# A graph layer on one core: where the edge count, the last store and the gathered blocks stand in the program

## The chip, the cores and the metric

The kernel runs on one core of one Trainium2 chip, in one launch. A core has TensorE (PE: matmuls, with a separate row PEld for its weight loads), VectorE (DVE), ScalarE (ACT), GpSimd (POOL) and SyncE (SP). They run side by side, each takes its own instructions strictly in order, and they wait for each other on semaphores. DMAs are issued from the queues of SP, ACT and POOL.

The metric is device time in microseconds (us): the median of several executions.

## The reference

One layer of a graph network over 6250 nodes of 128 features and 100,000 edges that are sorted by destination. Every edge carries its source's row through one of two weight matrices, by its type; the messages are summed by destination; the node's own row through a third matrix is added; then ReLU, the residual and a normalisation of each row.

```python
Xs = X[src]
m_data = Xs @ W_data.T + b_data
m_ctrl = Xs @ W_control.T + b_control
msg = jnp.where((edge_types == 0)[:, None], m_data, m_ctrl)
agg = jax.ops.segment_sum(msg, dst, num_segments=X.shape[0])
out = agg + (X @ W_self.T + b_self)
return jax.nn.relu(out)
# and around it
x = _layernorm(x + _L0_gnn_ref(x, ...), axis=-1)
```

## The kernel before

**Stages.** The nodes are cut into 49 blocks of 128. First a table of messages is built: every node times both edge matrices, split into three bf16 parts (384 columns a row), kept in SBUF (`m3`) and stored to DRAM (`table`). Then each destination block takes the edges that can belong to it, a window of 2304 sorted edges (KT = 18 columns of 128), and sums the messages of those edges. There are two ways of doing that.

- 35 blocks ("p", seven groups of five) go by *windows*. DVE and PE rank the edges of a group by the source's table block (`acc`, `slot`, `two`, `small`). The result, `packed`, is sent to DRAM and read back spread over all partitions (`rows`). Then each of 25 steps per block selects rows of `m3` with a matmul (`g_ps`, L754, steps "g"), ACT or DVE copies them out of PSUM as bf16 (`gs`, L769, steps "e"), and a second matmul adds them up by destination with a one-hot matrix (`agg`, L232, steps "s"). For the last group DVE shares those copies; before it only ACT does them. Edges that found no place are put on a short list and fetched by an indirect DMA into `mixed` (steps "over" to "spilled"). The step "full" (L701) takes what did not fit from that group's column of `counts`.
- 14 blocks ("g") are *gathered*: POOL fetches the message of each edge from `table` by indirect DMA (`msg`, L854, 14 x 18 of them, five buffers), and a matmul with a one-hot matrix (`hot_g`) adds them up (`agg_g`, steps "gm"). These are spread through the work of the windows.

Each finished block is summed from its three parts (`whole`, L153), gets the residual (`h_p` or `h_g`, L149) and its mean and variance (`stats`, L163, L164). `normalise` takes several blocks together, a piece of them: DVE writes `v` (L168), ACT takes its square root (L170), DVE makes `rstd` and `shift` in six small operations (L176 to L184), ACT applies them block by block (L190), and `store_out` stores the piece (L197, and L202 for the last, short block). The last two pieces of the windows are four blocks and one block of the last group; the last piece of the gathered blocks has four.

**What sets the order.** Nothing is ordered by hand. Each part is a generator that yields steps; a step has a name, a cost by engine and the steps that it needs. A planner (`Order.run`) keeps a clock for every engine: it finds the earliest start that any step could have, and among the steps of that engine that could start within 0.1 us of it takes the one with the lowest due time (`due`). The instructions of a step are then issued at that place of the program. So costs and due times only decide the order of each engine's instructions; on the chip they run as semaphores allow. Two constants set the due times of the second half: BLOCK (13.1) for a block of windows and PACE (1.75) for a gather. PACE is also the cost of a gather on POOL in the plan.

```python
if kind in ("p", "g") and i[0] in ("root", "rooted", "scale", "apply", "out"):
    n = i[1] + 1
    return BUILT + 10 + (BLOCK * sum(p[2] for p in PIECES[:n]) if kind == "p" else PACE * KT * GQ * n)
```

**The end.** `counts` (128 partitions x 8) holds how many edges every group, and the gathered blocks together, have taken in. After the last planned step a matmul with ones (L919) sums it over the partitions, DVE sums the eight columns (L921) and writes the integer `total` (L922). Then every engine loads `total` (L210) and branches (L211): if it isn't 100,000, a slower way over all edges (`sums_over_all`) runs; else it is jumped over, and the closing waits and barriers of the program follow (L1040). With these inputs it is jumped over.

Of the kernel before, what the change touches and what calls it, by code (L numbers as in the profile page):

```python
# [9 lines left out]
F32 = mybir.dt.float32  # L10
# [3 lines left out]
ALU = mybir.AluOpType  # L14
AX = mybir.AxisListType
# [4 lines left out]
P = 128  # L20
# [17 lines left out]
NPG = len(GROUPS)  # L38
NPB = sum(GROUPS)
NG = NB - NPB  # L40
STARTS = [sum(GROUPS[:i]) for i in range(NPG)]
# [59 lines left out]
def step(name, costs, *needs, lag=0.0):  # L101
    return as_tuple(name), costs, [as_tuple(n) for n in needs], lag
# [6 lines left out]
@with_exitstack  # L109
def kernel(  # L110
    ctx: ExitStack,
    tc: tile.TileContext,
    x: bass.AP,
    xt: bass.AP,
    edges: bass.AP,
    w: bass.AP,
    bias: bass.AP,
    out: bass.AP,
):

    nc = tc.nc  # L140
    dram = ctx.enter_context(tc.tile_pool(name="dram", bufs=1, space=DRAM))
    const = ctx.enter_context(tc.tile_pool(name="const", bufs=1))
    table = dram.tile([NT * P, D3], BF16, name="table")
    packed = dram.tile([NPB, NT * R], BF16, name="packed")
    total = const.tile([1, 1], I32, name="total")

    def finish(h, agg, xs):

        nc.vector.scalar_tensor_tensor(h, agg, 0.0, xs, op0=ALU.max, op1=ALU.add)  # L149

    def add_parts(agg, work):
        whole = work.tile([P, D], F32, name="whole")
        nc.vector.tensor_reduce(whole, agg.rearrange("p (i c) -> p c i", i=3), axis=AX.X, op=ALU.add)  # L153
        return whole

    def load_rows(b, work, name="xs", bufs=2):
        xs = work.tile([P, D], F32, name=name, bufs=bufs)
        nc.sync.dma_start(xs, x[b * P : (b + 1) * P, :])
        return xs

    def stats(mv, h, work):
        st = work.tile([P, 6], F32, name="st")
        nc.vector.bn_stats(st, h)  # L163
        nc.vector.bn_aggr(mv, st)  # L164

    def root(mv, n, work):
        v = work.tile([P, Q], F32, name="v")
        nc.vector.tensor_scalar_add(v[:, :n], mv[:, :n, 1], EPS)  # L168
        s0 = work.tile([P, Q], F32, name="s0")
        nc.scalar.activation(s0[:, :n], v[:, :n], AF.Sqrt)  # L170
        return v, s0

    def scale(mv, v, s0, n, work):

        r0 = work.tile([P, Q], F32, name="r0")
        nc.vector.reciprocal(r0[:, :n], s0[:, :n])  # L176
        q = work.tile([P, Q], F32, name="q")
        nc.vector.tensor_mul(q[:, :n], v[:, :n], r0[:, :n])
        nc.vector.tensor_add(q[:, :n], q[:, :n], s0[:, :n])
        rstd = work.tile([P, Q], F32, name="rstd")  # L180
        nc.vector.reciprocal(rstd[:, :n], q[:, :n])
        nc.vector.tensor_scalar_mul(rstd[:, :n], rstd[:, :n], 2.0)
        shift = work.tile([P, Q], F32, name="shift")
        nc.vector.scalar_tensor_tensor(shift[:, :n], mv[:, :n, 0], -1.0, rstd[:, :n],  # L184
                                       op0=ALU.mult, op1=ALU.mult)
        return rstd, shift

    def apply(h, rstd, shift, n):
        for j in range(n):
            nc.scalar.activation(h[:, j, :], h[:, j, :], AF.Identity,  # L190
                                 bias=shift[:, j : j + 1], scale=rstd[:, j : j + 1])

    def store_out(h, b0, n):
        n0 = b0 * P
        full = min(n, (N - n0) // P)
        if full:
            nc.sync.dma_start(  # L197
                out[n0 : n0 + full * P, :].rearrange("(b p) f -> p b f", p=P), h[:, :full, :]
            )
        if full < n:  # L200
            n1 = n0 + full * P
            nc.sync.dma_start(out[n1:N, :], h[: N - n1, full, :])  # L202

    norm = stats, root, scale, apply, store_out

    with ExitStack() as main:
        sums_over_windows(main, tc, x, xt, edges, w, bias, table, packed, total,
                          add_parts, finish, load_rows, norm)

    matched = nc.values_load(total[0:1, 0:1])  # L210
    with tc.If(matched != E), ExitStack() as rest:  # L211
        sums_over_all(rest, tc, xt, edges, w, bias, table, dram, finish, load_rows, norm)


def sums_over_windows(ctx, tc, x, xt, edges, w, bias, table, packed, total,
# [166 lines left out]

    LEAD, BUILT = 8.0, 76
    BLOCK = 13.1
    PACE = 1.75
    AHEAD, FIRST = 26.0, 20

    def due(kind, *i):
# [3 lines that stand above are left out]
        if kind in ("counted", "turned", "first"):  # L392
            return 5.0
        if kind == "idx":
            return BUILT - 4
        if kind in ("stores", "built"):
            return BUILT - 6
        each = (BUILT - 8 - LEAD) / NB
        if kind == "xt":
            return LEAD - 6 + each * at_part[i[0]]  # L400
        if kind == "er":
            return 5.0
        if kind in ("set", "slots"):
            return 14.0
        if kind == "counts":
            return 9.0 if i[0] == GROUPS[0] else 30.0
        if kind == "set2":
            return 40.0
        kinds = ("y", "yh", "y1", "ym", "y2", "yl")
        if kind in kinds:  # L410
            return LEAD + each * i[0] + kinds.index(kind)
        if kind == "table":
            return LEAD + each * (at_part[i[0]] + PARTS[i[0]]) + 14
        if kind in ("win", "xs", "agg", "o", "whole", "sum"):
            b = i[0]
            begun = BUILT + (BLOCK * b if b < NPB else PACE * KT * (b - NPB))
            if kind == "win":
                return due("fields", blocks[b][0]) - 8 if b < NPB else BUILT - 20
            if b >= NPB:
                return begun + {"whole": PACE * KT + 2, "sum": PACE * KT + 5}.get(kind, 0)  # L420
            return begun + {"whole": BLOCK + 0.5, "sum": BLOCK + 3}.get(kind, 0.3 * BLOCK)
        if kind in ("rows", "sel", "d", "g", "e", "s"):
            of = {"rows": 1, "sel": 1, "d": 2}.get(kind, NS)
            lead = {"rows": -9, "sel": -3, "d": -1, "g": 0, "e": 1, "s": 2}[kind]
            return BUILT + BLOCK * (i[0] + (i[1] / of if len(i) > 1 else 0)) + lead
        if kind in ("gh", "gm", "msg"):
            k = i[1] * CH if kind == "gh" else i[1]
            return BUILT + PACE * (i[0] * KT + k) + {"msg": 0, "gh": 2, "gm": 5}[kind]
        n = GROUPS[i[0]]
        end = BUILT + BLOCK * STARTS[i[0]] - (AHEAD if i[0] else FIRST)  # L430
        span = BLOCK * n if i[0] else 34.0
        begun = end - span
        if kind == "fields":
            return begun - 8
        if kind == "hot":
            return begun + span * i[1] * KC / KT - 4
        if kind in ("tri", "rank", "rest"):
            return begun + span * i[1] / KT + {"tri": 0, "rank": 0.5, "rest": 1}[kind]
        if kind in ("two", "v"):
            c, k = (i[1], 0) if kind == "two" else divmod(i[1], KC)  # L440
            return begun + span * (c + 1) * KC / KT + (2 if kind == "two" else 3 + 0.3 * k)
        return end + ("vs", "vd", "to", "over", "pos", "codes", "posed", "list", "listed",
                      "spilled", "full").index({"packed": "vs"}.get(kind, kind))
# [370 lines left out]
    def normalise(pieces, last):  # L814

        for grp, (get, b0, q0, n) in enumerate(pieces):
# [6 lines left out]
            scales = scale(mv, v, s0, n, work)  # L823
            yield step((last, "apply", grp), {"A": 0.28 * n}, (last, "scale", grp))
            apply(h, *scales, n)
            yield step((last, "out", grp), {"S": 0.3}, (last, "apply", grp))
            store_out(h, b0, n)


    gathered = [(j, k) for j in range(NG) for k in range(KT)]  # L830
# [59 lines left out]
            stats(mv[:, j % GQ, :], h[:, j % GQ, :], work)  # L890


    late = ps_g = None

    def close_build():
# [8 lines left out]
        spread(), select(), finish_blocks(),  # L904
        normalise([(lambda g=g: (hs_[g], mvs[g]), STARTS[g] + q0, q0, n) for g, q0, n in PIECES], "p"), add_up(), gather(), evict(), to_hots(), bucket_hots(),
        multiply(), take(0, "yh", "y"), leave(0, "y1", "yh"),
        take(1, "ym", "y1"), leave(1, "y2", "ym"), take(2, "yl", "y2"), constants(), store(), close_build(),
        finish_gathered(), gathered_sums(), gathered_hots(), gather_rows(), gathered_fields(),
        normalise([(lambda i=i: kept[i], NPB + i * GQ, 0, min(GQ, NG - i * GQ))
                   for i in range(-(-NG // GQ))], "g"),  # L910
# [3 lines left out]
        own_of(list(range(NPB, NB)), lambda b: ("gm", b - NPB, 0)),  # L914
    ], due)


    total_ps = ps_a.tile([P, 512], F32, name="small")
    T.matmul(total_ps[:1, : NPG + 1], ones[:, 0:1], counts, start=True, stop=True)  # L919
    total_f = work.tile([1, 1], F32, name="total_f")  # L920
    V.tensor_reduce(total_f, total_ps[:1, : NPG + 1], axis=AX.X, op=ALU.add)  # L921
    V.tensor_copy(total, total_f)  # L922


def sums_over_all(ctx, tc, xt, edges, w, bias, table, dram, finish, load_rows, norm):
# [118 lines left out]
```

## Time and profile before

| what | us |
|---|---|
| median of 3 executions | 632.7 (629.24 to 637.61) |
| the profiled execution: its own time | 545.63 |
| its span, first to last instruction | 543.9 |
| its mean granted TensorE clock | 0.989 |
| first and last g_ps matmul | 79.9 and 530.0 |
| first and last msg gather of POOL | 89.0 and 520.4 |
| last agg_g matmul starts | 527.3 |
| `total` written | 536.0 |
| last store (out<-h_p) issued by SP | 536.5 |

The profile is of one execution, taken by the hardware profiler. A row of a group view names the line, the engine, the operation, and what is written from what, by the program's names. A row of a chain or of a timeline begins with its start and its length in us; "issue" is time in which the engine waited for nothing that the profile shows. A wait is put down to what came last. The engine names with a q (PEldq, DVEq, SPq) are the engines' sequencers, which handle branches, register loads and semaphores.

Over the whole span the page gives busy shares: PE 93%, PEld 81%, DVE 78%, ACT 78%, POOL 54%; and for the 16 DMA engines a mean of 146 GB/s.

### The profile page before, as it was taken

How to read it: one execution, taken by the hardware profiler on the slowest of the kernel's cores; microseconds unless marked ns; L12 is line 12 of the kernel's file. 1: busy time of each engine (PE TensorE's matmuls, PEld its weight loads, DVE VectorE, ACT ScalarE, POOL GpSimd, SP SyncE). 2: the span in 40 equal slices, each digit the busy share in tenths (PEclk: the TensorE clock that was granted, in tenths of full speed). 3: DMA queues.
4: the chain of work that ended last, by engine and by line, in shares of the span. 5: the costliest groups of instructions: out<-in, count | busy, mean ns of one | idle time of the engine just before them, and what ended most of it. 6: DMA issues, size and time to landing. Idle time of an engine off the chain costs nothing.

```text
span 543.9 us, 26402 instructions
## 1 busy us (share of the span) xinstructions
PE 504.0 (93%) x11222; PEld 440.7 (81%) x11222; DVE 425.9 (78%) x958; ACT 422.6 (78%) x1012; POOL 296.4 (54%) x267
## 2 busy tenths in 40 slices
PE   4899978999899999999999999999999999979990
PEld 3555538799789999898998989989988898869990
DVE  4677679778887889888799788988798766867872
ACT  6745556697778888879879797798789987978782
POOL 1000004776766667767487576676677556676610
PEclk9999989999999999999999999999999999999996
DMA  3466984444454443645445445444355542646211
GB/s 110 134 178 189 285 278 136 147 142 124 138 149 154 140 128 128 174 124 156 139 137 153 134 140 169 155 147 118 114 179 169 160 140 62 194 143 189 91 46 30
DMA packets 60934, 79.20 MB, mean 146 GB/s; under 512 B 15761, under 2 KB 51372, under 8 KB 60808
## 3 DMA queue, kind: packets, MB, share of 16 engines
q1 hardware_dynamic: 47253, 48.95, 28.0%
q0 software_dynamic: 12400, 25.08, 16.9%
q10 hardware_dynamic: 1154, 3.41, 1.8%
q8 instruction: 89, 1.46, 1.1%
q14 instruction: 38, 0.30, 0.2%
HBM read 64.35 MB, written 13.05 MB: 142 GB/s over the span
## 4 chain that ended last, share of the span: by engine, by line
PE 72%; DMA 11%; DVE 9%; ACT 3%; issue 2%; SPq 1%; POOL 1%; DVEq 0%; ACTq 0%; POOLq 0%
PE agg L232 23%; PE g_ps L754 22%; PE acc L232 8%; PE small L600 7%; PE agg_g L232 7%; DMA msg<-table,idx 5%; DMA rows<-packed 5%; PE y L460 2%; DVE hot_st L546 2%; DVE slot L563 1%; ACT gs L769 1%; ACT h_p L190 1%; PE y L478 1%; DVE rows L725 1%; ACT h_g L190 1%
## 5 line engine op out<-in xcount | busy, mean ns | idle before, releaser
L769 ACT CAST gs<-g_ps 128x384 bf16<-128x384 f32 x807 | 334.3, 495 | 71.3 <-PE g_ps L754 58.2
L854 POOL DMA_INDIRECT msg<-table,idx x252 | 285.9, 1135 | 133.7 <-PE g_ps L754 64.9
L754 PE MATMUL g_ps<-m,rows 128*32 128x384 bf16 x3430 | 319.1, 331 | 0.0
L232 PE MATMUL agg<-gs,hot_d 128*32 128x384 bf16 x3360 | 298.2, 329 | 3.7 <-ACT gs L769 3.2
L754 PEld LDWEIGHTS <-rows 128*32 128x32 bf16 x3430 | 187.2, 136 | 16.8 <-issue 10.1
L232 PEld LDWEIGHTS <-hot_d 128*32 128x32 bf16 x3500 | 188.8, 137 | 11.4 <-issue 6.8
L232 PE MATMUL agg_g<-msg,hot_g 128*32 128x384 bf16 x1008 | 108.0, 329 | 7.2 <-DMA msg<-table,idx 6.8
L563 DVE TENSOR_REDUCE slot<-acc 128x5 bf16<-128x490 f32 x126 | 83.5, 663 | 36.3 <-PE acc L232 28.3
L739 DVE TENSOR_TENSOR hot_d<-count,to 128x1664 bf16<-128x1664 bf16 x70 | 74.7, 1068 | 8.1 <-PE agg L232 7.9
L600 PE MATMUL small<-hot_st,two 128*32 128x98 bf16 x1260 | 72.5, 290 | 0.0
L600 PEld LDWEIGHTS <-two 128*32 128x32 bf16 x1260 | 59.1, 117 | 3.6 <-issue 1.4
L232 PEld LDWEIGHTS <-hot_g 128*32 128x32 bf16 x1008 | 53.0, 124 | 11.0 <-issue 9.4
L232 PE MATMUL acc<-hot_st,rest 128*32 128x490 bf16 x476 | 54.4, 376 | 7.9 <-DVE slot L563 7.8
L232 PE MATMUL acc<-hot_st,tri 128*32 128x490 bf16 x504 | 60.5, 375 | 1.1 <-DVE hot_st L546 1.1
L471 ACT CAST m<-y 128x512 bf16<-128x512 f32 (+1 forms) x75 | 40.6, 580 | 26.1 <-PE y L478 18.8
L694 POOL DMA_INDIRECT mixed<-table,row_i x7 | 8.2, 1169 | 86.5 <-PE g_ps L754 80.5
L546 DVE TENSOR_TENSOR hot_st<-count,st_b 128x2940 bf16<-128x2940 bf16 x21 | 41.9, 1999 | 7.7 <-PE small L600 6.3
L725 DVE TENSOR_SCALAR rows<-rows,pid 128x3136 bf16<-128x3136 bf16 x35 | 37.2, 1062 | 6.0 <-DMA rows<-packed 6.0
L232 PEld LDWEIGHTS <-rest 128*32 128x32 bf16 x476 | 21.7, 97 | 17.8 <-issue 16.3
L460 PE MATMUL y<-w_sb,xt 128*128 128x256 f32 x98 | 31.3, 407 | 1.8 <-DMA xt<-in_xt 1.8
L153 DVE TENSOR_REDUCE whole<-agg 128x128 f32<-128x384 f32 x35 | 19.3, 552 | 12.3 <-PE agg L232 9.2
L769 DVE CAST gs<-g_ps 128x384 bf16<-128x384 f32 x33 | 18.0, 555 | 12.9 <-PE g_ps L754 12.4
(140 smaller groups left out, 426.2 us busy)
## 6 DMA issues: line engine op xcount, KB each, us to landing
rows<-packed SPq DMA_DIRECT2D x35, 784.0 KB
table<-m SPq DMA_DIRECT2D x10, 768.0 KB
msg<-table,idx POOLq DMA_INDIRECT x252
xt<-in_xt ACTq DMA_DIRECT2D x5, 512.0 KB
xt_p<-in_xt SPq DMA_DIRECT2D x35, 64.0 KB
xs_p<-in_x SPq DMA_DIRECT2D x35, 64.0 KB
out<-h_p SPq DMA_DIRECT2D x6, 320.0 KB
table<-m SPq DMA_DIRECT2D x2, 480.0 KB
```

The costliest lines, as they stand in the source:

```text
L153: nc.vector.tensor_reduce(whole, agg.rearrange("p (i c) -> p c i", i=3), axis=AX.X, op=ALU.add)
L232: T.matmul(out[c : c + 32], lhsT[:, c : c + 32], rhs, **flags)
L460: T.matmul(y[:, j, :], xts[g][:, b + j - at_part[g], :], w_sb[:, : 2 * D], start=j == 0, stop=False, skip_group_check=True)
L471: A.copy(part_of(b, n, i), ys[b][:, :n, :].rearrange("p b (t c) -> p t b c", t=2))
L546: V.tensor_tensor(hot, counted[n][:, None, 1 : NT + 1, :].to_broadcast([P, KC, NT, n]), fields[grp][2][:, c * KC : c * KC + KC, None, :].t ...
L563: V.tensor_reduce(slots[grp][:, k, :], by_q, axis=AX.X, op=ALU.max)
L600: T.matmul(vt[c0 : c0 + R, q // 2, :], two[:, k % KC, i, :, q], hot[:, k % KC, :, q], start=k == 0 and q < 2, stop=k == KT - 1, skip_group ...
L725: V.tensor_scalar(rows[b], rows[b], pid1, None, op0=ALU.is_equal)
L739: V.tensor_tensor(hot, counted[DC][:, :, :n], places[grp][:, q, None, c * DC : c * DC + n].to_broadcast([P, P, n]), op=ALU.is_equal)
L754: T.matmul(g_ps[t * R : (t + 1) * R, :D3], rows[b][:, :, s], m3[:, s, :], start=True, stop=True)
L769: (A.copy if e == "A" else V.tensor_copy)(gs[at], g_tiles.pop((b, g))[at, :D3])
L854: G.indirect_dma_start(out=msgs[j, k], out_offset=None, in_=table[:, :], in_offset=bass.IndirectOffsetOnAxis(ap=idx[:, j, k : k + 1], axis=0),
```

## The change

Three edits to the end of the program.

1. `PACE` goes from 1.75 to 1.68.
2. The sum of `counts` becomes two planned steps, "total" on PE and "totalled" on DVE, in a generator `add_counts` of their own. They need the last group's "full" and "listed", the first one-hot tile of the second block of the last group, and the gathered blocks' count ("idx"). Their due time is that of the last block of windows. The same three instructions after the plan go away.
3. `store_out` takes the queue as an argument. The last piece of the windows is stored from ACT's queue, planned on ACT with a cost of 0.4; all other pieces from SP's, as before.

```diff
-    def store_out(h, b0, n):
+    def store_out(h, b0, n, by=nc.sync):
         n0 = b0 * P
         full = min(n, (N - n0) // P)
         if full:
-            nc.sync.dma_start(
+            by.dma_start(
...
-    PACE = 1.75
+    PACE = 1.68
...
+        if kind in ("total", "totalled"):
+            return BUILT + BLOCK * (NPB - 1)
...
-            yield step((last, "out", grp), {"S": 0.3}, (last, "apply", grp))
-            store_out(h, b0, n)
+            at_end = last == "p" and grp == len(pieces) - 1
+            yield step((last, "out", grp), {"A": 0.4} if at_end else {"S": 0.3}, (last, "apply", grp))
+            store_out(h, b0, n, nc.scalar if at_end else nc.sync)
...
+    def add_counts():
+        yield step("total", {"T": 0.2}, ("full", NPG - 1), ("listed", NPG - 1), ("d", STARTS[-1] + 1, 0), "idx")
+        total_ps = ps_a.tile([P, 512], F32, name="small")
+        T.matmul(total_ps[:1, : NPG + 1], ones[:, 0:1], counts, start=True, stop=True)
+        yield step("totalled", {"V": 0.35}, "total")
+        total_f = work.tile([1, 1], F32, name="total_f")
+        V.tensor_reduce(total_f, total_ps[:1, : NPG + 1], axis=AX.X, op=ALU.add)
+        V.tensor_copy(total, total_f)
...
-        take(1, "ym", "y1"), leave(1, "y2", "ym"), take(2, "yl", "y2"), constants(), store(), close_build(),
+        take(1, "ym", "y1"), leave(1, "y2", "ym"), take(2, "yl", "y2"), constants(), store(), close_build(), add_counts(),
...
-
-    total_ps = ps_a.tile([P, 512], F32, name="small")
-    T.matmul(total_ps[:1, : NPG + 1], ones[:, 0:1], counts, start=True, stop=True)
-    total_f = work.tile([1, 1], F32, name="total_f")
-    V.tensor_reduce(total_f, total_ps[:1, : NPG + 1], axis=AX.X, op=ALU.add)
-    V.tensor_copy(total, total_f)
```

## The prediction

> **What bounds the kernel now.** I read the page's head first, then the stretches by time, then the chain of waits of the last microseconds, then the instructions of the line that ends the program.
>
> The head says that TensorE is the engine to watch:
>
> ```profile
> span 543.9 us, 26402 instructions
> ...
> PE 504.0 (93%) x11222; PEld 440.7 (81%) x11222; DVE 425.9 (78%) x958; ACT 422.6 (78%) x1012; POOL 296.4 (54%) x267
> ```
>
> The stretches say where TensorE stops being the bound: it is busy for 9.96 us of the 10 us of the last block of windows, and for 0.31 us of the 13 us after it. The third column is PE's busy time, then PEld, DVE, ACT, POOL.
>
> ```profile
> 521.30:531.30 10.00, 9.96 (x226) 8.46 (x218) 7.85 (x25) 8.52 (x22) 0.05 (x1) 1.00 0.13 38
> 531.00:544.00 13.00, 0.31 (x10) 0.15 (x5) 3.47 (x19) 2.33 (x7) 0.00 (x0) 0.68 0.12 31
> ```
>
> So there are two different limits: about 450 us in which TensorE sets the pace, and a tail of 12.6 us (531.3 to 543.9) in which it has nothing to do. The chain of waits tells the first half of the tail (start, length, what):
>
> ```profile
> 531.38 0.54 DVE whole L153
> 531.92 0.10 DVE r L176
> ...
> 532.84 0.17 DVE shift L184
> 533.01 0.03 issue
> 533.04 1.65 ACT h_g L190 x4
> 534.68 0.10 ACT s L170
> ...
> 535.97 0.49 ACT h_p L190
> ```
>
> The last block (h_p) has to be summed, scaled and stored. But six small DVE operations for the last gathered blocks (r L176 to shift L184, 531.83 to 533.00) stand between its two steps on DVE, and four ACT operations for the same blocks (h_g, 1.65 us) stand ahead of its square root on ACT. Both are work of other blocks on the last block's path.
>
> The second half is the end of the program: after `total` is written (L922, 536.04 + 0.14), all engines load it (L210) and branch on it (L211). The view of that line (operation, count, ns min/median/max, start):
>
> ```profile
> L211 ACTq COMPARE_BRANCH  x1: 45/45/45, 536.7 to 536.7; - x1
> L211 DVEq COMPARE_BRANCH  x1: 76/76/76, 536.8 to 536.8; - x1
> L211 PEldq COMPARE_BRANCH  x1: 4171/4171/4171, 536.8 to 536.8; - x1
> L211 DVEq EVENT_SEMAPHORE  x1: 21/21/21, 540.5 to 540.5; - x1
> L211 PEldq EVENT_SEMAPHORE  x1: 51/51/51, 541.1 to 541.1; - x1
> ```
>
> TensorE's branch takes 4.17 us; DVE's takes 0.08 us, but its next instruction starts 3.58 us later. TensorE ended its sums at 531.3 and could have done this from then on; it sat waiting for `total` until 536.2, because DVE counts last of all.
>
> [...] 4.17 us on PE, 3.58 us on DVE after L211, against 0.40 us on ACT[...]. [...] SP issued the last store at 536.49, 0.03 us after ACT's last result (535.97 + 0.49). So the move of the store is worth about nothing by itself.
>
> **The change part by part.** The changed kernel's instruction order, which can be read from its build, says what moves.
>
> *Gathered blocks sooner (PACE 1.75 to 1.68).* It adds and removes no sum. Due times and planned costs of the 252 gathers shrink, so the last of the 14 gathered blocks ends about two window blocks sooner in TensorE's order: the last two blocks have no agg_g left. On DVE the gathered scale now stands in the block before last, on ACT the four h_g activations stand some 40 instructions before the end, and SP stores h_g before the last h_p. From the tail: DVE's second step (h_p, L149) started at 532.92; it can now start 0.05 us after `whole` ended (531.92), at 531.97: 0.95 us less. From there to `shift` took 3.02 us (532.92 to 535.94), of which ACT's square root was late: v ended at 533.94, the root began at 534.59 behind h_g, a gap of 0.65; in the gathered chain just before, the gap from v to the root was 0.12. So 0.53 us less again. Sum: **1.5 us**; shift then ends at 534.45.
>
> *Edges counted earlier.* The matmul of counts (two passes, 0.20 us of PE time together), the reduction (0.15) and the cast (0.14) move into the stretch of block 31, behind work that is not waiting: +0.2 us on PE at the most, +0.3 on DVE, which is idle for a fifth of that stretch (DVE 78%). On the path they leave 0.24 us (535.94 to 536.18). Their larger effect is on the branches. PE loads at 531.3 (0.49), branches (4.17) and is done at 536.0 instead of 541.0. SP and POOL, whose last DMAs are issued long before the end, load and branch while the sums still run. DVE is now last: load 534.5 to 535.0, branch, 3.58 us of fetch, next instruction at 538.7 instead of 540.5. ACT: apply ends at 534.95, store issue 0.4, load 0.46, 0.45 for its branch and what follows: 536.3. What is behind them: the closing semaphores of SP took from 540.7 to 542.1; those that do not wait for DVE can now run early. After DVE's release SP needs 0.2 us for the last ones and then the 1.86 us that ran from 542.08 to 543.93 before: 538.75 + 0.2 + 1.86 = 540.8. If the 0.9 us between SP's last two drains in that stretch also lies beside DVE's fetch, it is 539.8. Bounds of the unknown: [...] 2 to 3.7 us for it; the end then lies between 538.5 and 540.9. I take 540.3: **3.6 us** from the tail in all, 1.5 of them from the first part and 2.1 from the second.
>
> *Last store on ACT's queue.* The issue (0.36 us on SP) goes to ACT; nothing is behind it but ACT's load of `total`, which ends 2.4 us ahead of DVE's fetch. SP is freed to branch early, counted above. By itself **0**; from -0.1 (a hop saved) to +0.1.
>
> *What it costs further up.* Two things, both on TensorE's side. First, with gathered sums closer together, POOL's spacing shrinks from 1.72 us ((520.4 - 89.0) / 251) to about 1.65; a gather is busy 1.135 us and the next follows 0.30 later, so 1.43 is its floor. That holds, with less slack. TensorE waited 6.8 us in all for gathered rows (8 waits); by nearness I allow 0 to +4 more, and take +0.5. Second, the two last blocks lose their fill. TensorE then needs 49.5 x 0.1625 + 0.6 = 8.6 us for one block; by the order ACT has about 16 evictions (0.413 each), 4 applies (0.41) and a root in each, 8.5 us, and DVE in block 33 has 8 evictions (0.56), two finishes (1.4 each), a hot_d (1.06) and a scale (1.2), 9.5 us. So DVE or ACT can hold TensorE up by 0 to 1.5 us; I take +0.3. The remaining reshuffle (hundreds of DVE and ACT instructions change places within a few microseconds) has no sign that I can read: 0, with -2 to +3.
>
> **Sum.** -3.6 + 0.5 + 0.3 + 0.2 = -2.6, with the likely case between -5 and -1. The profiled execution took 545.63 us (span 543.9 and 1.7 around it), so it would be about 543. The median of the runs shown is 632.7, 87 us above that execution, which no part of the page explains: its clock is 0.989. [...] So I carry the tail's gain, 3 to 3.5 us, to the median: **629.5 us**.
>
> **The rivals.**
>
> *It does nothing (chance 0.2).* For it: the tail's gain is smaller than the spread of the three runs (8.4 us), and half rests on fetches that may simply end as late because the last branch is still taken at the end by DVE. Then only 1 us is left and the reshuffle takes it: 632 us.
>
> *Slower: TensorE waits for gathered rows (0.13; over the 2% bound 0.06).* TensorE takes its instructions in order. If the order now asks for agg_g before its rows have landed, every g_ps and agg behind it stands too, and ACT's evictions with them. The place is agg_g L232, the price what the landing is late; the whole path from 89 to 512 us has 252 such points. For it: the chain of waits already has 5% (27 us) of msg DMA[...]. Against it: five buffers, 6.8 us of real waits, POOL 54% busy. It decides from 0.02 us for each gather (5 us: the gain is gone, 635 us); at 0.06 us for each it is 15 us, 645 to 648, past the bound.
>
> *Larger gain from the order itself (0.07; over the bound 0.04).* TensorE's waits for `slot` (7.8 us) and for gathered rows (6.8 us) could shrink if gathers land in better places: 14.6 at the most, 618 us.
>
> *As forecast (0.6):* 625 to 632.
>
> **How the numbers follow.** A measurement of this kernel can tell about 2% (12.7 us) from no change. The main case and the empty case lie within it, and so does half of each outer case: 0.04 faster, 0.89 same, 0.07 slower. The three runs shown lie from -3.5 to +4.9 around their median; with that and the bounds above the range is 622 to 638.5, which leaves out most of the outer cases and no more than 2 in 10.
>
> **What would show it.** Right: DVE's second step of the last block follows `whole` within 0.1 us; no h_g after TensorE's end; PE's branch starts near TensorE's last sum and its 4 us lie beside other work; DVE's next instruction after L211 comes last; from TensorE's end to the span's end 9 us instead of 12.6. Wrong: waits of agg_g for msg above 10 us; PE idle in the last two blocks; TensorE's last sum later than 533; or the span's end still 5 us after the last apply plus the fetch of an engine that I took to be early.

## The result, and the profile after

| | before | after |
|---|---|---|
| median of 20 executions, us | 631.87 (629.24 to 637.83) | 630.13 (627.54 to 634.76) |
| ratio of after to before | | 0.9954, 95% interval 0.9932 to 0.9976 |
| profiled execution, span, us | 543.9 | 626.6 |
| its granted clock | 0.989 | 0.985 |

In this measurement the change makes the kernel 0.2 to 0.7% faster. The spans of the two profiles must not be subtracted: as far as can be told they are from different chips, and before takes 549.8 us in the median on one chip of the runs and 631.9 and 632.5 on the two others (the last section). What can be compared is the tail, from the end of TensorE's last agg matmul to the end of the span: its steps up to the last store come at the same times on all three chips of the runs (the table below: `shift` ends at 3.06 or 3.07 us, or at 4.63 or 4.64, by the value of PACE). Three stretches of the trace after: the last two blocks of windows and the tail (third column PE busy, then PEld, DVE, ACT).

```profile
598.70:608.60 9.90, 9.56 (x220) 8.13 (x213) 8.47 (x26) 8.89 (x23) 0.00 (x0) 1.00 0.10 26
608.60:617.75 9.15, 8.91 (x198) 7.22 (x189) 6.38 (x20) 7.73 (x20) 0.00 (x0) 1.00 0.12 34
617.75:626.60 8.85, 0.00 (x0) 0.00 (x0) 2.44 (x11) 0.69 (x2) 0.00 (x0) 0.72 0.05 15
```

The tail is 8.8 us; it was 12.6. TensorE is no longer busy in all of its last two blocks, though: 18.47 us of the 19.05 us of these two stretches. The chain of waits through the tail after:

```profile
617.80 0.57 DVE whole L153
618.37 0.02 issue
618.39 0.30 DVE h_p L149
...
619.26 0.16 DVE v L168
619.42 0.02 issue
619.45 0.21 ACT s L170
...
620.66 0.17 DVE shift L184
```

`whole` is followed at once by the residual (0.02 us), and `v` by its root (0.02 us): h_g is gone from both places. The line that ends the program, after:

```profile
L211 SPq EVENT_SEMAPHORE  x8: 17/17/17, 618.4 to 624.8; - x8
...
L211 POOLq COMPARE_BRANCH  x1: 54/54/54, 592.0 to 592.0; - x1
L211 SPq COMPARE_BRANCH  x1: 50/50/50, 615.8 to 615.8; - x1
L211 PEldq COMPARE_BRANCH  x1: 3387/3387/3387, 618.0 to 618.0; - x1
L211 DVEq COMPARE_BRANCH  x1: 76/76/76, 621.3 to 621.3; - x1
L211 PEldq EVENT_SEMAPHORE  x1: 51/51/51, 621.4 to 621.4; - x1
L211 DVEq EVENT_SEMAPHORE  x1: 21/21/21, 624.2 to 624.2; - x1
```

POOL branches 26 us before TensorE ends, SP 2 us before, and TensorE's own 3.4 us lie beside the last block's scaling. DVE's first instruction after its branch is now the last of the engines', at 624.2. SP's own came long before, but the last of its eight waits of this line starts at 624.8. It is taken here for the wait for the landing of the last store: in the three profiles of the full change and in no_branch it comes 0.4 to 0.6 us after that store's last packet.

**Who comes last.** The program ends in a barrier that all engines have to reach; the row DRAIN of the closing line (L1040, after L1047) gives for each engine when it first stands there. Before:

```profile
L1040 SPq DRAIN  x3: 7/13/130, 542.1 to 543.4; - x3
...
L1040 DVEq DRAIN  x2: 10/14/17, 540.6 to 543.4; - x2
L1040 PEldq DRAIN  x2: 8/8/8, 541.2 to 543.4; - x2
```

After:

```profile
L1047 SPq DRAIN  x3: 7/13/130, 625.6 to 626.2; - x3
L1047 PEldq DRAIN  x2: 8/8/8, 621.5 to 626.0; - x2
...
L1047 DVEq DRAIN  x2: 10/14/17, 624.3 to 626.0; - x2
```

SP comes last, before as after, and in every run of the table. Behind its branch it has eight waits (of the line L211) and a row of twelve more semaphore instructions. Before, this row began as soon as SP's own jump was done and went on without a pause, one every 0.06 to 0.1 us, so it waited for nobody:

```profile
L211 SPq EVENT_SEMAPHORE  x8: 17/17/17, 540.7 to 541.2; - x8
```

TensorE, with its branch of 4.17 us, stood at the barrier 0.9 us before SP (541.2 against 542.1).

### The profile page after: what moved, and what is told of

It reads as the page before. It is cut to its first block, busy times and chain, and to the rows that moved or that the text cites. A ratio compares the mean times of both kernels' runs of the same rounds, so it can differ in the third digit from the quotient of the medians.

```text
span 626.6 us, 26397 instructions
## 1 busy us (share of the span) xinstructions
PE 550.4 (88%) x11222; PEld 441.2 (70%) x11222; DVE 429.4 (69%) x962; ACT 424.7 (68%) x1008; POOL 292.8 (47%) x267
## 4 chain that ended last, share of the span: by engine, by line
PE 80%; ACT 7%; issue 5%; DVE 4%; DMA 2%; SPq 1%; another core or an unknown queue 0%; POOL 0%; ACTq 0%; DVEq 0%; POOLq 0%
PE agg L232 27%; PE g_ps L756 26%; PE acc L232 8%; PE agg_g L232 8%; PE small L602 7%; ACT gs L771 5%; PE y L462 2%; ACT h_p L190 1%; DMA rows<-packed 1%; DVE slot L565 1%; PE y L480 1%; DVE hot_st L548 1%; ACT h_g L190 1%; PE y L464 0%; DMA xt<-in_xt 0%
## 5 line engine op out<-in xcount | busy, mean ns | idle before, releaser
L756 PE MATMUL g_ps<-m,rows 128*32 128x384 bf16 x3430 | 330.8, 334 | 19.2 <-ACT gs L771 11.6
L232 PE MATMUL agg<-gs,hot_d 128*32 128x384 bf16 x3360 | 304.4, 338 | 27.8 <-ACT gs L771 12.9
L232 PEld LDWEIGHTS <-hot_d 128*32 128x32 bf16 x3500 | 198.9, 137 | 66.7 <-issue 56.4
L602 PE MATMUL small<-hot_st,two 128*32 128x98 bf16 x1260 | 70.9, 290 | 1.4 <-issue 1.3
L602 PEld LDWEIGHTS <-two 128*32 128x32 bf16 x1260 | 56.8, 118 | 6.7 <-issue 4.6
L232 PE MATMUL acc<-hot_st,tri 128*32 128x490 bf16 x504 | 58.8, 376 | 1.0 <-DVE hot_st L548 0.9
L232 PEld LDWEIGHTS <-hot_g 128*32 128x32 bf16 x1008 | 51.4, 125 | 4.9 <-issue 3.0
```

The source lines that it names most:

```text
L232: T.matmul(out[c : c + 32], lhsT[:, c : c + 32], rhs, **flags)
L602: T.matmul(vt[c0 : c0 + R, q // 2, :], two[:, k % KC, i, :, q], hot[:, k % KC, :, q], start=k == 0 and q < 2, stop=k == KT - 1, skip_group ...
L756: T.matmul(g_ps[t * R : (t + 1) * R, :D3], rows[b][:, :, s], m3[:, s, :], start=True, stop=True)
```

## The experiments

Each is the change, a part of it, or a variant. The first four ran on a chip on which before takes 549.8 us, the others on two chips on which it takes 631.9 and 632.5; a ratio is always to before on the same chip. The row "after" is the result's own profile and ratio. The table is worked out from the traces: times in us after the end of TensorE's last agg matmul. "Next" is the start of an engine's first instruction after its branch; the stretch from the branch to it is called the engine's fetch (the last section has what the traces show of it). "SP's waits" is the start of the last of SP's eight waits behind it. The times of a row are of one execution: the two of counts and store end 0.1 us apart, the three of the full change up to 0.54, so that half a microsecond between two tails is little.

| kernel | shift ends | last store issued | PE next | DVE next | SP next | SP's waits | end (tail) | ratio, 95% interval |
|---|---|---|---|---|---|---|---|---|
| before_again | 4.64 | 5.19 | 9.75 | 9.19 | 9.39 | 9.92 | 12.60 | |
| pace_only | 3.06 | 3.62 | 8.31 | 7.60 | 7.91 | 8.44 | 10.49 | 1.0010 (0.9988 to 1.0033) |
| counts_only | 4.63 | 5.18 | 3.90 | 8.41 | 8.78 | 9.31 | 11.96 | 0.9967 (0.9943 to 0.9990) |
| counts_store | 4.64 | 5.19 | 3.64 | 8.40 | 7.25 | 7.92 | 9.83 | 0.9943 (0.9922 to 0.9963) |
| store_only | 4.63 | 5.19 | 9.79 | 9.09 | 8.47 | 9.00 | 11.71 | 0.9986 (0.9952 to 1.0020) |
| no_act_store | 3.06 | 3.62 | 3.64 | 7.17 | 7.82 | 8.35 | 10.59 | 1.0011 (0.9988 to 1.0035) |
| after | 3.07 | 3.62 | 3.65 | 6.42 | 0.64 | 7.06 | 8.82 | 0.9954 (0.9932 to 0.9976) |
| after_same_chip | 3.07 | 3.63 | 3.78 | 6.95 | 0.64 | 6.53 | 8.28 | 0.9975 (0.9956 to 0.9993) |
| after_third | 3.07 | 3.62 | 3.69 | 6.46 | 0.73 | 6.58 | 8.35 | 0.9982 (0.9959 to 1.0005) |
| counts_store_2 | 4.64 | 5.20 | 4.00 | 8.31 | 7.26 | 7.84 | 9.74 | 0.9955 (0.9930 to 0.9979) |
| no_branch | 3.06 | 3.62 | | | | 5.20 | 6.13 | 0.9934 (0.9910 to 0.9957) |
| pace_172 | 3.06 | 3.62 | 4.35 | 6.76 | 2.66 | 6.26 | 8.45 | 0.9994 (0.9965 to 1.0024) |
| pace_1745 | 3.07 | 3.63 | 3.80 | 6.84 | 4.80 | 6.78 | 8.54 | 0.9888 (0.9834 to 0.9943) |

**before_again.** No edit.

> The kernel before, unchanged, for a second profile: its first profiled execution took 545.6 us where 20 others took 629 to 638. Theory: that one execution was out of the ordinary and a new one takes 629 to 638 us at a clock of 0.98, with TensorE's gaps between weight loads spread over the whole window stage (about 150 us of gaps over 0.35 us, as in the changed kernel's trace, against 63 us in the first profile of before). Rival: the changed order brought these gaps, then before's new trace has 60 to 70 us of them. In both, the tail from the end of TensorE's last agg matmul to the span's end is 12.6 us, plus or minus 0.5.

Neither theory held as it stands. The second profile is like the first one: 547.65 us, a tail of 12.60 us, and gaps in the same few places, and so are the 50 executions beside it (544.71 to 553.37). So it isn't one execution out of the ordinary: this chip is faster, and the first profile, as far as can be told, came from such a chip. The gaps are as few as the rival had it, but the changed order doesn't bring them. Counted here from the end of one weight load to the start of the next, where it is over 0.35 us, they sum to 35 us in before_again, 36 in pace_only and 34 in counts_store, all on this chip, and to 99 in after and 101 in store_only, which has the order of before, on others.

**One part at a time: pace_only, counts_only, counts_store.**

```diff
pace_only, against before
-    PACE = 1.75
+    PACE = 1.68
counts_only, against after
-    PACE = 1.68
+    PACE = 1.75
-            at_end = last == "p" and grp == len(pieces) - 1
+            at_end = False
counts_store, against after
-    PACE = 1.68
+    PACE = 1.75
```

> PACE 1.68 alone; counts still summed last, last store from SP. Theory (two gains that add): the last block's path loses h_g's scale and applies, 1.5 us, so the tail is 11.1 us against 12.6; the branch of TensorE still comes after total and still takes about 4 us on the path. Rival (the last block's path carries the whole gain): the tail is 9 us, as in the full change (8.8). Ratio to before 0.997 plus or minus 0.003; above 1.002 if gathers closer together cost TensorE more than 2.5 us.

> Edges counted early alone; PACE 1.75, last store from SP. Theory: TensorE and POOL branch early, but SP can load total only after it has issued the last store and then needs its own fetch of some 3.2 us, so only 1.0 us is gained: tail 11.5 us. Rival (the prediction's sum, in which the store's queue is worth nothing): 2.1 us gained, tail 10.5 us.

> Edges counted early and the last store from ACT, PACE 1.75. Theory: SP is now free to branch before the sums end, and DVE's fetch and the store's landing come last, so the tail is 10.4 us, 1.1 less than with the counts alone. Rival (the store's queue is worth nothing): as with the counts alone, within 0.3 us.

PACE alone ends `shift` 1.58 us earlier, as worked out (1.5), and takes 2.1 us from the tail, 0.6 more than its theory. SP issues the last store 1.57 us sooner, and so it branches sooner, and its row follows. TensorE's branch still comes after `total` (next at 8.31 us), but TensorE stands at the barrier at 8.5 and SP at 9.3. The ratio is 1.0010, above the 0.997 that was expected: what the tail gains is lost before it.

The counts alone gain 0.65 us, less than the theory's 1.0 and hardly more than two executions of one kernel can differ by. Of counts_only:

```profile
L211 SPq EVENT_SEMAPHORE  x8: 17/17/17, 544.2 to 544.7; - x8
...
L211 PEldq COMPARE_BRANCH  x1: 3631/3631/3631, 535.6 to 535.6; - x1
...
L211 SPq COMPARE_BRANCH  x1: 50/50/50, 541.5 to 541.5; - x1
L211 DVEq EVENT_SEMAPHORE  x1: 21/21/21, 543.8 to 543.8; - x1
```

TensorE branches at 535.6, near its last sum, and is out of the way. But SP can branch only after it has issued the last store; its own fetch (541.5 to 544.2) ends last, and its row of closing waits begins only then. SP branches no sooner than before (6.11 us); what is gained is that its fetch takes 2.6 us instead of 3.2. With the store on ACT, of counts_store:

```profile
L211 SPq COMPARE_BRANCH  x1: 50/50/50, 537.0 to 537.0; - x1
...
L211 DVEq EVENT_SEMAPHORE  x1: 21/21/21, 540.7 to 540.7; - x1
```

SP branches right after its store of h_g, and the tail falls by another 2.1 us, to 9.83 (9.74 when it was run again). The rival, that the queue is worth nothing, is refuted here.

**The other halves: no_act_store, store_only.** 

```diff
no_act_store, against after
-            at_end = last == "p" and grp == len(pieces) - 1
+            at_end = False
store_only, against after
-    PACE = 1.68
+    PACE = 1.75
-        ... close_build(), add_counts(),
+        ... close_build(),
+    total_ps = ps_a.tile([P, 512], F32, name="small")
...
+    V.tensor_copy(total, total_f)
```

> PACE 1.68 and edges counted early, last store from SP. Theory: SP branches only after the last store and needs 2.6 us of fetch then, so the tail is 9.5 to 10.3 us, 0.7 to 1.5 more than the full change. Rival (the store's queue is worth nothing, as predicted): 8.8, within 0.3 us.

> The last store from ACT alone; PACE 1.75, counts summed last. Theory: by itself it is worth nothing, because all branches still wait for total and TensorE's branch (4.2 us) comes last: tail 12.4 to 12.7 us, ratio 1.000 plus or minus 0.002. Rival (the queue is worth about 2 us wherever it stands, as it was behind the early counts): tail 10.5 us. Up to the last store its order is that of the kernel before.

Without the store on ACT, the other two edits have a tail of 10.59 us, no better than PACE alone (10.49): then SP's next instruction comes at 7.82, and the early counts are worth nothing. The tail is 0.3 us above the theory's bound, and 1.8 to 2.3 above the full change. The store alone leaves TensorE's branch where it was (next at 9.79) and by the theory should have been worth nothing; its tail is 11.71, 0.9 less. The theory had the wrong engine last: without the store SP loads `total` and branches 0.7 us sooner (5.41 instead of 6.12), and its next comes at 8.47 instead of 9.39. TensorE is now 0.1 us ahead of SP at the barrier. In each run with the branch the closing also holds a pause of 0.4 to 1.0 us, not always at the same instruction (in before between SP's first two DRAINs, in store_only on POOL); what makes it isn't known. A gain of 0.9 us is less than the interval of this kernel's ratio.

**What the branch still costs: no_branch.** It leaves out the slower way over all edges, and with it the load of `total` and the branch.

```diff
-    matched = nc.values_load(total[0:1, 0:1])
-    with tc.If(matched != E), ExitStack() as rest:
-        sums_over_all(rest, tc, xt, edges, w, bias, table, dram, finish, load_rows, norm)
```

> The full change without the branch and the slower way behind it (the kernel then never reads total; the slower way isn't taken with these inputs, so the output is the same). Theory: in the full change DVE's fetch and the store's landing behind the fetched pages still cost about 2 us, so the tail is 6.3 to 7 us and the ratio 0.994. Rival (all the branch's cost is hidden by now): 8.5 us or more.

The tail is 6.13 us, so in the full change the branch still costs 2.2 to 2.7 us. DVE's fetch (next at 6.4 to 6.95 us) is not what they consist of: DVE stands at the barrier 0.3 to 1.4 us ahead of SP. The last store is issued at 3.62 or 3.63 us in no_branch and in all three of the full change. Without the branch SP's wait for its landing ends 1.6 us later, and with it 2.9 to 3.4 us later: 1.3 to 1.9 us. The other 0.8 us are the row of semaphore instructions, which SP has behind that wait when there is a branch, and nearly all ahead of it when there is none.

The store's last packets of 512 bytes end at 4.8 us without the branch and at 6.0 to 6.5 with it, in a stretch in which pages of instructions are fetched by DMA as well (in the trace after, one of 16,384 bytes from 5.05 to 6.01 us and two of 8192 between 4.59 and 6.17); without the branch no page is fetched in the tail. The same can be seen between two runs that issue this store from SP at 3.62 us: in pace_only its packets end at 4.8 us and the first page starts at 5.0, in no_act_store the pages start at 4.6 and the packets end at 6.5. That the pages hold the store up is inferred from this; which packets stood behind which wasn't shown.

**The same change again, and without PACE: after_same_chip, counts_store_2, after_third.** No new edits.

> The full change on the chip of the experiments. Theory (PACE 1.68 costs TensorE what it wins at the end): the tail is 8.8 us (3.8 less than before), but some 2.6 us are lost further up, so the ratio to before is 0.998 plus or minus 0.003, no better than counts and store with PACE 1.75 (0.9943). Rival (the loss with PACE alone was chance): 0.9925, the tails added up.

> Edges counted early and store from ACT with PACE 1.75, again, beside the full change on one chip. Theory (PACE 1.68 wins 1 to 1.5 us at the end and loses more than that before it): ratio to before 0.9945 plus or minus 0.0025, lower than the full change's. Rival (PACE pays): the full change is lower by 0.002.

> The full change once more on the same chip as counts and store with PACE 1.75. Theory: 0.9965 plus or minus 0.002, as in the two measurements before (0.9954, 0.9975), above counts and store alone. Rival: below it.

The full change has 0.9954, 0.9975 and 0.9982 in three measurements, 0.9970 in the mean: 1.9 us of 632. Its tail is 3.8 to 4.3 us shorter than the 12.6 of before, so about 2 us are lost before the tail. Counts and store with PACE 1.75 have 0.9943 and 0.9955, some 3 us, on two chips, which is about what their tails say (2.8 and 2.9 less): nothing is lost, as far as intervals of 1.1 to 1.5 us to either side can tell. On the chip that had both, counts and store had 0.9955 and the full change 0.9982; the intervals overlap, so that PACE 1.68 costs more than it brings is likely, not shown.

**Other values of PACE: pace_172, pace_1745.** The change with `PACE = 1.72`, and with `PACE = 1.745`.

> The full change with PACE 1.72: in its order h_g's scale and applies are clear of the last block's path too, but the gathered sums still fill TensorE until the middle of the block before last. Theory: the tail is that of the full change (8.8 us) and the loss further up is smaller, ratio 0.993 plus or minus 0.003. Rival (any sooner PACE costs the same 2.6 us): 0.998.

> The full change with PACE 1.745, the smallest step of those built whose order has h_g's scale ahead of the last block's whole. Gathered sums fill TensorE almost to the end, as before. Theory: a tail of 8.3 to 9 us with less lost before it, ratio 0.993 plus or minus 0.003. Rival: each new order of the steps gives or takes some 3 us by itself, and the ratio is anywhere from 0.990 to 1.000, whatever the tail.

Both tails are like the full change's (8.45, 8.54). The ratios are 0.9994 and 0.9888. So the theory of a cost that shrinks with the step falls with 1.72, which loses nearly 4 us before the tail (give or take 2). With 1.745 the kernel takes 7.1 us less, 4.1 of them in the tail; the other 3 lie within its interval (3.5 us to either side), so that 1.745 gains anything before the tail isn't shown. That each value gives the planner another order of thousands of steps, worth some us by itself, fits these runs best; with four values it isn't proven. pace_1745 is faster than both kernels; its interval (six executions) does not touch that of the full change on the same chip, but it does that of counts and store. Its last two blocks by stretches:

```profile
596.00:607.20 11.20, 10.39 (x234) 8.87 (x237) 7.06 (x15) 7.60 (x18) 4.73 (x5) 1.00 0.19 50
607.20:617.10 9.90, 9.62 (x210) 7.80 (x202) 7.83 (x28) 9.22 (x26) 0.00 (x0) 1.00 0.10 28
```

POOL (the fifth busy time) still gathers in the block before last, where it had ended in the full change.

## Why the prediction was right

629.5 us were forecast and 630.13 measured. That they agree within 0.6 us is in part luck. The 629.5 starts from 632.7, the median of three executions, and twenty have 631.87. The prediction's own sum was -2.6 us, and it carried 3.2 to the median, leaving out the costs further up; these came, some 2 us of them. The gain was 1.7 us by the medians, 2.9 by the ratio of that measurement and 1.9 by the mean of three ratios. The range of 622 to 638.5 us held "no effect" as well.

What stands is that the tail would be some 3.6 us shorter, because h_g leaves the last block's path and the branches move beside other work. What was wrong is which engine ends the program, and with it two terms of the sum, which made up for each other.

- *TensorE's and DVE's branches at the end of the path.* The prediction read the end from TensorE's 4.17 us and DVE's 3.58, and took SP's closing row for something behind them. SP's row waited for neither: it began at 540.7, when SP's own jump was done, and SP came to the barrier 0.9 us after TensorE. SP branched last because it issues the last store first.
- *The tail, 3.6 us less.* Measured 3.8 to 4.3.
- *h_g off the last block's path, 1.5 us.* `shift` ended 1.58 us earlier, by the two steps named: the residual follows `whole`, the root follows `v`.
- *Edges counted earlier, 2.1 us.* Mis-sized: alone 0.65, and 0 beside PACE 1.68. The step counted SP among the engines that "load and branch while the sums still run". That isn't so while SP issues the last store: alone, its next instruction came at 8.78 us, behind DVE's 8.41.
- *The store on ACT's queue, 0 by itself.* Alone, its tail was 0.9 us shorter (one execution); and it is what lets the early counts pay: 2.1 us between counts_only and counts_store, 1.8 to 2.3 between no_act_store and the full change. The prediction booked these 2 us under the counts. A store moved off a queue was priced by the issue time saved, and not by what is behind it on that queue, which is the branch and its 2.5 to 3.3 us of fetch.
- *DVE's fetch comes last, the end between 538.5 and 540.9 on the old scale.* The 2 to 3.7 us that were allowed for DVE's fetch were an estimate; in after it took 2.8. On the old scale the three profiles of the full change end at 539.6 to 540.1, as forecast. DVE's next is the last of the engines', but the end hangs on a thing not named: SP's wait for the landing of the last store. The span ends 1.75 to 1.77 us after that wait in all three, while DVE's next lies from 0.6 us ahead of it to 0.4 behind it.
- *Gathers closer together, +0.5.* The waits of agg_g for gathered rows did not grow: 7.7 us before, 6.8 with PACE alone, from these lines of before_again and pace_only:

```profile
PE agg_g L232 <- DMA msg<-table,idx: 7.7, 8, 1.7
```

```profile
PE agg_g L232 <- DMA msg<-table,idx: 6.8, 10, 1.6
```

- *The last two blocks without their fill, +0.3 of 0 to 1.5.* Measured about +1.4: from the end of one block's last agg matmul to that of the next they took 9.70 and 9.25 us with PACE alone, 9.64 and 9.56 in before_again; but ten gathered sums (10 x 0.1625 = 1.6 us) were gone from them: 18.95 against 19.20 - 1.6. PACE alone loses 2.7 us before the tail, give or take 1.2; where the rest of them goes wasn't found. How TensorE comes to wait can be seen in the trace after, on ACT:

```profile
603.19 1.63 ACT L771 CAST gs<-g_ps 128x384 bf16<-128x384 f32 x4 [0.17 <-PE g_ps L756]
604.68 1.67 ACT L190 ACTIVATE h_g<-h_g,shift,rstd 128x128 f32<-128x128 f32 x4
606.23 1.24 ACT L771 CAST gs<-g_ps 128x384 bf16<-128x384 f32 x3
```

  and in its chain of waits, where the h_g that left the tail stands on the path again, with TensorE waiting for the copy behind it:

```profile
604.82 0.99 ACT h_g L190 x3
605.81 0.04 issue
605.85 0.50 ACT h_g L190
606.35 0.38 ACT gs L771
606.72 0.04 issue
606.77 0.39 PE agg L232 x4
```

- *The remaining reshuffle, -2 to +3 without a sign.* The runs agree with such a width: 4 us lost before the tail for 1.72, and for 1.745 anything from none to several gained. It is the largest uncertainty of the forecast and was rightly left in the range; as a term it was too small beside the 3.6.
- *The 87 us between profile and median.* The granted clock doesn't explain them: the 20 executions of the changed kernel, of 627.5 to 634.8 us, had clocks of 0.978 to 0.989, and the profiled execution of before, of 545.63 us, had 0.989. The difference goes with the chip (the last section). That the tail's gain stays the same in the longer executions was an estimate: the three profiled ones of the full change, of 628.3 to 630.0 us, have tails 3.8 to 4.3 us shorter than before at 545.6 and 547.7 us, but no longer execution of before was profiled.

## What to carry to other kernels

The branch at the end of this program still costs 2.2 to 2.7 us in the changed kernel. Where a program ends in one, price each engine's jump by the gap between its branch and its next instruction, look which engine comes last to the closing barrier, and not which has the longest jump, and have every engine's last work, and the value that it branches on, done early enough that the jump lies beside something else. The last store took SP 0.36 us to issue in before, and its move to ACT was worth 2.1 us behind the early counts, because SP had its jump behind it: look what stands behind a queue's last DMA. Parts that only pay together must be taken out one at a time and also put in one at a time. Where a planner orders thousands of steps, a constant changed for the end changes the middle too (PACE 1.72 lost nearly 4 us there): measure the end by its own stretch, and try neighbouring values of the constant before crediting the idea.

## What the runs showed of the hardware

**Chips differ by 15% for this program.** The same kernel, before, takes 549.8 us in the median of 50 executions on one chip and 631.9 and 632.5 on two others, with granted clocks of 0.987 in the median on the first and 0.979 and 0.980 on the others. Each chip was measured at one time only, so something else that differed between these times isn't excluded. store_only has the order of before up to its last store, so its trace can be laid beside before_again's. The copies take the same time on both, 485 and 484 ns in the median (first before_again, then store_only):

```profile
L769 ACT CAST gs<-g_ps x807: 455/485/618, 80.8 to 531.8; 128x384 bf16<-128x384 f32 x162
```

```profile
L771 ACT CAST gs<-g_ps x807: 457/484/584, 81.1 to 616.9; 128x384 bf16<-128x384 f32 x162
```

But on the second chip TensorE waits more for them, and for nothing that the profile shows:

```profile
PE agg L232 <- ACT gs L769: 3.2, 6, 1.0
```

```profile
PE agg L232 <- ACT gs L771: 12.8, 22, 1.6
...
PE agg L232 <- issue: 10.6, 29, 1.0
PE g_ps L756 <- issue: 10.4, 21, 1.7
...
PE g_ps L756 <- ACT gs L771: 7.2, 16, 1.0
```

These waits make up some 38 of the 84 us between the two spans; the others lie in a longer busy time of TensorE, 552.6 us instead of 504.7, for the same number of matmuls. The cause stays open. With 84 us between two chips, spans of this program can only be compared if they are of the same chip.

**A taken branch held an engine for 0.1 to 4.3 us.** TensorE's took 3.4 to 4.0 us when it branched ahead of DVE and 4.2 to 4.3 when all branched together; DVE's next instruction came 2.8 to 3.6 us after its branch, SP's 2.5 to 3.3, ACT's 0.4, POOL's 0.1 to 0.5. The stretches are called fetches because DMA queues of the kind "instruction" are at work in them: these queues move six pages in the tail after (two of 16,384 bytes and four of 8192), and none in that of no_branch. In after (us from the end of the last agg matmul) one page moves from -0.98 to -0.47, within SP's stretch (-1.86 to 0.64), two between 1.21 and 2.15, within TensorE's branch (0.20 to 3.59), and three between 4.59 and 6.17, within DVE's stretch (3.62 to 6.42). That an engine waits for such a page is inferred from this; which page is whose wasn't shown. The size may depend on who else fetches: SP's took 2.6 us in counts_only, where TensorE's was out of the way, and 3.2 in before; but in no_act_store, where it was out of the way too, it took 3.2, so this isn't shown.
